# Masked attention on one core: scores and product with V moved from halves of TensorE's array to 64x64 quarters

## The chip, the cores and the metric

The kernel runs on one core of one Trainium2 chip. The metric is the device time of one execution in microseconds (us); several executions are quoted as their median. All runs quoted here are in the fast state. The profile is of one further execution. Engines are named as the profile does: PE (TensorE's matmuls), PEld (its weight loads), DVE (VectorE), ACT (ScalarE), POOL (GpSimd), SP (the queue that issues transfers).

## The reference, cut to what matters

```python
x = _layernorm(x + graph_convolution_with_batchnorm(x, adj, ...))     # layer 0
qkv = x @ W                                                           # layer 1: 4 heads of 64
scores = einsum('bhid,bhjd->bhij', q, k) / sqrt(64) + where(adj == 0, -inf, 0)
out = einsum('bhij,bhjd->bhid', softmax(scores), v)
x = _layernorm(x + out)
```

x is 8 x 2048 x 256 in fp32. The change touches layer 1 alone, which takes the last 2631 of the 4072 us.

## The kernel before

The work is cut into 64 units: a batch, a pair of heads (128 of the 256 columns) and a chunk of 512 queries. A unit has 16 key tiles `j` of 128 keys, taken two at a time in 8 steps `g`. Scores run two steps ahead of the product.

```python
ps_s = ctx.enter_context(tc.tile_pool(name="ps_s", bufs=2, space=PSUM))   # 2 banks each
ps_o = ctx.enter_context(tc.tile_pool(name="ps_o", bufs=2, space=PSUM))   # 1 bank each
ps_m = ctx.enter_context(tc.tile_pool(name="ps_m", bufs=2, space=PSUM))   # 1 bank each

# scores(u, g)                               two heads on the array's upper and lower 64 rows
ps = ps_s.tile([P, 2, CH], F32, name="ps_s")
for h in range(2):
    hs = slice(h * HD, (h + 1) * HD)
    nc.tensor.matmul(ps[:, h, :], kt[hs, j * P : (j + 1) * P], qt[hs, k * CH : (k + 1) * CH],
                     start=True, stop=True)
# ...
nc.vector.tensor_tensor(pt, ps, mask[...], op=ALU.subtract)              # DVE, 1.2 us
nc.scalar.activation(pt, pt, AF.Exp, scale=2.0**MASK_EXP)                # ACT, 1.05 us
nc.gpsimd.tensor_add(accs[u, q], accs[u, q], pt)                         # POOL, 2.36 us, 14 a unit

# weigh(u, g)                                two heads on the array's left and right 64 columns
for h in range(2):
    nc.tensor.matmul(outs[u][h * HD : (h + 1) * HD, :], qkv[b, hp][2][:, j, h * HD : (h + 1) * HD],
                     pt[:, h, :], start=(j == 0), stop=(j == NT - 1))

def finish_copy(u):                          # the way out, one step after the unit's last product
    ot = ap_.tile([P, CH], F32, name="ot")
    nc.scalar.copy(ot, outs[u])
```

Beside these steps stand projections, transposes and two layer norms per chunk. One belongs to the next batch's rows, one to the finished rows. Each layer norm has this chain, and it matters below:

```python
nc.vector.tensor_scalar(rs, mv[:, :, 1], EPS, None, op0=ALU.add)         # DVE
nc.gpsimd.tensor_tensor(rs, rs, mhalf[:, :TPC], op=ALU.pow)              # POOL
nc.vector.scalar_tensor_tensor(nm, mv[:, :, 0], -1.0, rs, ...)           # DVE
nc.scalar.activation(t[:, i, :], t[:, i, :], AF.Identity, bias=nm, scale=rs)   # ACT, four times
```

The compiler chooses the order of each engine's instructions, and the traces show that an edit in one place can move instructions elsewhere (an instance at 2118 us is given at the end of the part on why the prediction was wrong). They also show an engine waiting for the next instruction in its order while a later one could run (VectorE at 3944 us, below); the text calls that order the engine's queue.

## Time and profile before

| | us |
|---|---|
| time, median of 3 runs | 4072.4 |
| attention, from first score to end | 2631 |
| PE busy, share of the whole | 97% |
| POOL busy in the attention's steady period | 273 of 324 |

"Steady period" is the stretch of eight units of one batch, which repeats every 323.8 us. Read busy shares as follows. A TensorE that is 97% busy by modelled ends can still hide pauses, so the argument here rests on the times at which matmuls start. The prediction shows the lines.

### The profile page before, as it was taken

The page shows a single profiled execution, that of the slowest core. Times are in us where ns is not written, and L with a number is a line of the kernel's source. Part 1 is how long each engine was busy: PE and PEld are TensorE (multiplying, and loading weights), DVE is VectorE, ACT ScalarE, POOL GpSimd, SP SyncE. Part 2 cuts the span into 40 slices and gives each one's busy share as a digit, 9 for nine tenths or more (in the row PEclk, how much of TensorE's full clock was granted, in tenths as well). Part 3 has the DMA queues.
Part 4 walks back from the last instruction along what each step waited for, and adds up shares of the span by engine and source line. Part 5 has one row for each costly group of instructions (what it writes and reads, how often), then busy time and mean ns, then how long its engine had stood idle before and what let it go on. Part 6 is the DMA issues. An engine that isn't in the chain of part 4 may idle for free. (4 is left out here: it accounts for less than half of the span.)

```text
span 4072.3 us, 38096 instructions
## 1 busy us (share of the span) xinstructions
PE 3938.3 (97%) x14626; PEld 1559.8 (38%) x14626; DVE 1867.2 (46%) x2525; ACT 1665.7 (41%) x2077; POOL 2285.9 (56%) x1083
## 2 busy tenths in 40 slices
PE   7999999999989989999999999999999999999997
PEld 5444444444434433333333333333333333333332
DVE  5211111111124435665565665665656666556565
ACT  5000000000024345555555555555555555545554
POOL 0011101110100038887887887888888888788897
PEclk8999999999999989999999999999999999999998
DMA  5111101110147620000010000000000000000000
GB/s 217 64 45 52 52 31 49 47 49 31 47 158 230 208 68 21 25 28 26 16 42 21 21 32 21 32 32 21 32 21 32 26 27 27 26 6 26 6 1 22
DMA packets 94426, 197.28 MB, mean 48 GB/s; under 512 B 7072, under 2 KB 73120, under 8 KB 83872
## 3 DMA queue, kind: packets, MB, share of 16 engines
q1 hardware_dynamic: 94240, 194.80, 13.7%
q8 instruction: 117, 1.92, 0.2%
q14 instruction: 69, 0.57, 0.0%
HBM read 106.70 MB, written 88.08 MB: 48 GB/s over the span
## 5 line engine op out<-in xcount | busy, mean ns | idle before, releaser
L466 POOL TENSOR_TENSOR acc<-acc,pt 128x1024 f32<-128x1024 f32 x768 | 1814.2, 2362 | 329.1 <-ACT pt L459 286.5
L453 DVE TENSOR_TENSOR pt<-ps_s,mask 128x1024 f32<-128x1024 f32 x1024 | 1209.4, 1217 | 943.5 <-PE ps_s L446 908.4
L459 ACT ACTIVATE pt<-pt 128x1024 f32<-128x1024 f32 x1024 | 1066.5, 1054 | 816.7 <-DVE pt L453 796.2
L446 PE MATMUL ps_s<-qt,kt 64*128 64x512 f32 x4096 | 1041.1, 620 | 47.8 <-DVE pt L453 47.7
L475 PE MATMUL ps_o<-pt,v 128*64 128x512 f32 x4096 | 1013.0, 607 | 2.9 <-ACT pt L459 2.9
L209 PE MATMUL pa<-at,xb 128*128 128x512 f32 x2048 | 885.5, 592 | 0.0
L446 PEld LDWEIGHTS ps_s<-qt,kt 64*128 64x128 f32 x4096 | 351.3, 186 | 640.1 <-issue 339.9
L187 POOL TENSOR_SCALAR xb<-xb,dinv 128x256 f32<-128x256 f32 x112 | 103.0, 948 | 863.9 <-DMA xb<-in_x_dram 851.8
L209 PEld LDWEIGHTS pa<-at,xb 128*128 128x128 f32 x2048 | 389.0, 190 | 487.2 <-issue 480.0
L475 PEld LDWEIGHTS ps_o<-pt,v 128*64 128x64 f32 x4096 | 252.0, 136 | 637.6 <-issue 539.8
L242 ACT ACTIVATE h<-ph,b1s 128x512 f32<-128x512 f32 x128 | 87.9, 687 | 993.9 <-PE ph L235 993.9
L228 DVE TENSOR_TENSOR ag<-pa,dbc 128x512 f32<-128x512 f32 x64 | 44.3, 692 | 769.8 <-PE pa L209 769.8
L464 POOL TENSOR_TENSOR acc<-pt 128x1024 f32<-128x1024 f32 x128 | 302.3, 2362 | 71.4 <-ACT pt L459 70.2
L414 PE MATMUL pm<-x1t,wq 128*128 128x512 f32 x512 | 255.7, 624 | 0.5 <-ACT x1t L398 0.5
L295 PE MATMUL py<-h,w2s 128*128 128x512 f32 x512 | 223.6, 599 | 13.7 <-ACT h L287 13.7
L235 PE MATMUL ph<-ag,w1s 128*128 128x512 f32 x512 | 225.1, 592 | 0.0
L88 POOL TENSOR_TENSOR rs<-rs,mhalf 128x4 f32<-128x4 f32 (+1 forms) x2 | 1.7, 870 | 378.9 <-DVE rs L87 378.9
L350 ACT ACTIVATE x<-x,ln_nm,ln_rs 128x256 f32<-128x256 f32 x256 | 132.6, 588 | 100.0 <-DVE ln_nm L346 100.0
L243 DVE BATCH_NORM_STATS2 st<-h 128x6 f32<-128x512 f32 x128 | 88.8, 694 | 148.5 <-ACT h L242 148.5
L414 PEld LDWEIGHTS pm<-x1t,wq 128*128 128x128 f32 x512 | 88.4, 191 | 165.7 <-issue 104.9
L295 PEld LDWEIGHTS py<-h,w2s 128*128 128x128 f32 x512 | 98.4, 193 | 138.9 <-issue 119.1
L287 ACT ACTIVATE h<-h,sh,sc 128x512 f32<-128x512 f32 x128 | 93.3, 801 | 134.9 <-DMA h<-h_d 125.3
(78 smaller groups left out, 1780.7 us busy)
## 6 DMA issues: line engine op xcount, KB each, us to landing
h_d<-h SPq DMA_DIRECT2D x32, 1024.0 KB, 3.9
h<-h_d SPq DMA_DIRECT2D x32, 1024.0 KB, 5.9
a<-in_adj_dram SPq DMA_DIRECT2D x16, 1024.0 KB, 8.3
xb<-in_x_dram SPq DMA_DIRECT2D x32, 512.0 KB, 3.9
y_d<-y SPq DMA_DIRECT2D x32, 512.0 KB, 6.4
yt<-y_d SPq DMA_DIRECT2D x32, 512.0 KB, 3.3
x<-in_x_dram SPq DMA_DIRECT2D x32, 512.0 KB, 3.8
x_d<-x SPq DMA_DIRECT2D x32, 512.0 KB, 2.8
```

The costliest lines, as they stand in the source:

```text
L187: nc.gpsimd.tensor_scalar(t4[:, j, :], t4[:, j, :], dv, None, op0=ALU.mult)
L209: nc.tensor.matmul(pa, xs[b][m // TPC][:, m % TPC, d * P : (d + 1) * P], at[:, m, c * CH : (c + 1) * CH], start=(m == 0), stop=(m == NT - 1),)
L235: nc.tensor.matmul(ph, w1s[:, d, f * P : (f + 1) * P], ag[:, d, :], start=(d == 0), stop=(d == ND - 1),)
L295: nc.tensor.matmul(py, w2s[:, f, o * P : (o + 1) * P], h[:, f, :], start=(f == 0), stop=(f == NH - 1),)
L350: nc.scalar.activation(t[:, i, :], t[:, i, :], AF.Identity, bias=nm[:, i : i + 1], scale=rs[:, i : i + 1],)
L414: nc.tensor.matmul(pm, wq[:, d, wcols], xt[:, d, cols], start=(d == 0), stop=(d == ND - 1))
L446: nc.tensor.matmul(ps[:, h, :], kt[hs, j * P : (j + 1) * P], qt[hs, k * CH : (k + 1) * CH], start=True, stop=True,)
L453: nc.vector.tensor_tensor(pt, pss[j - g * GJ], mask[:, j, None, k * CH : (k + 1) * CH].to_broadcast([P, 2, CH]), op=ALU.subtract,)
L459: nc.scalar.activation(pt, pt, AF.Exp, scale=2.0**MASK_EXP)
L464: nc.gpsimd.tensor_add(accs[u, q], probs[u, j - 1], pt)
L466: nc.gpsimd.tensor_add(accs[u, q], accs[u, q], pt)
L475: nc.tensor.matmul(outs[u][h * HD : (h + 1) * HD, :], qkv[b, hp][2][:, j, h * HD : (h + 1) * HD], pt[:, h, :], start=(j == 0), stop=(j == ...
```

## The change

Its intent: scores use the array as two row halves, the product as two column halves, so the array changes its tiling twice a step. On quarters both have one tiling. A product over quarters splits its 128 keys over two row tiles, which write to two PSUM banks; they are added on the way out. Two banks per output leave room for one output buffer in place of two.

```diff
-        ps_o = ctx.enter_context(tc.tile_pool(name="ps_o", bufs=2, space=PSUM))
+        ps_o = ctx.enter_context(tc.tile_pool(name="ps_o", bufs=1, space=PSUM))
...
-                for h in range(2):
-                    nc.tensor.matmul(ps[:, h, :], kt[hs, j * P : (j + 1) * P], qt[hs, ...], ...)
+                for q in range(2):
+                    for h in range(2):
+                        nc.tensor.matmul(ps[q * HD : (q + 1) * HD, h, :], kt[hs, c0 : c0 + HD], qt[hs, ...], ...)
...
-                outs[u] = ps_o.tile([P, CH], F32, name="ps_o")
+                outs[u] = ps_o.tile([P, 2, CH], F32, name="ps_o")
...
                 for h in range(2):
-                    nc.tensor.matmul(outs[u][h * HD : (h + 1) * HD, :], qkv[b, hp][2][:, j, ...], pt[:, h, :], ...)
+                    for q in range(2):
+                        nc.tensor.matmul(outs[u][h * HD : (h + 1) * HD, q, :], qkv[b, hp][2][qs, j, ...], pt[qs, h, :], ...)
...
-            nc.scalar.copy(ot, outs[u])
+            nc.scalar.copy(ot, outs[u][:, 0, :])
+            nc.vector.tensor_add(ot, outs[u][:, 1, :], ot)
```

More of the change, by code (lines that the diff above doesn't have):

```diff
@@ L443, in scores @@
                 ps = ps_s.tile([P, 2, CH], F32, name="ps_s")
-                for h in range(2):
-                    hs = slice(h * HD, (h + 1) * HD)
-                    nc.tensor.matmul(
-                        ps[:, h, :], kt[hs, j * P : (j + 1) * P], qt[hs, k * CH : (k + 1) * CH],
-                        start=True, stop=True,
-                    )
+                for q in range(2):
+                    for h in range(2):
+                        hs = slice(h * HD, (h + 1) * HD)
+                        c0 = j * P + q * HD
+                        nc.tensor.matmul(
+                            ps[q * HD : (q + 1) * HD, h, :],
+                            kt[hs, c0 : c0 + HD],
+                            qt[hs, k * CH : (k + 1) * CH],
+                            start=True,
+                            stop=True,
+                        )
                 pss.append(ps)
@@ L474, in weigh @@
                 for h in range(2):
-                    nc.tensor.matmul(
-                        outs[u][h * HD : (h + 1) * HD, :],
-                        qkv[b, hp][2][:, j, h * HD : (h + 1) * HD],
-                        pt[:, h, :],
-                        start=(j == 0),
-                        stop=(j == NT - 1),
-                    )
+                    for q in range(2):
+                        qs = slice(q * HD, (q + 1) * HD)
+                        nc.tensor.matmul(
+                            outs[u][h * HD : (h + 1) * HD, q, :],
+                            qkv[b, hp][2][qs, j, h * HD : (h + 1) * HD],
+                            pt[qs, h, :],
+                            start=(j == 0),
+                            stop=(j == NT - 1),
+                        )
         def finish_copy(u):
             ot = ap_.tile([P, CH], F32, name="ot")
-            nc.scalar.copy(ot, outs[u])
+            nc.scalar.copy(ot, outs[u][:, 0, :])
+            nc.vector.tensor_add(ot, outs[u][:, 1, :], ot)
             outs[u] = ot
```

## The prediction

> **What bounds the kernel now.** I read the page first, then the windows by stage, then the order of the weight loads on TensorE, then the ends of a few units, and last the table of waits. The page's busy shares and costliest groups:
>
> ```profile
> PE 3938.3 (97%) x14626; PEld 1559.8 (38%) x14626; DVE 1867.2 (46%) x2525; ACT 1665.7 (41%) x2077; POOL 2285.9 (56%) x1083
> ...
> L466 POOL TENSOR_TENSOR acc<-acc,pt 128x1024 f32<-128x1024 f32 x768 | 1814.2, 2362 | 329.1 <-ACT pt L459 286.5
> L453 DVE TENSOR_TENSOR pt<-ps_s,mask 128x1024 f32<-128x1024 f32 x1024 | 1209.4, 1217 | 943.5 <-PE ps_s L446 908.4
> L459 ACT ACTIVATE pt<-pt 128x1024 f32<-128x1024 f32 x1024 | 1066.5, 1054 | 816.7 <-DVE pt L453 796.2
> L446 PE MATMUL ps_s<-qt,kt 64*128 64x512 f32 x4096 | 1041.1, 620 | 47.8 <-DVE pt L453 47.7
> L475 PE MATMUL ps_o<-pt,v 128*64 128x512 f32 x4096 | 1013.0, 607 | 2.9 <-ACT pt L459 2.9
> ```
>
> The reader should see that TensorE is busy 97% and that the two groups the change touches are half of that. Both use half the array per matmul, and both already run two at a time: 4096 records of 620 ns would be 2540 us, yet their union is 1041. Each fp32 matmul leaves two records, so 2048 matmuls of each kind. The attention runs from 1441 us (first score) to the end, some 2620 us. Busy ends are modelled, though, so a busy TensorE can hide gaps. Starts cannot. A long chain in one shape (the aggregation) starts one record every 0.43 us:
>
> ```profile
> 900.24 0.19 PEld L209 LDWEIGHTS pa<-at,xb 128*128 128x128 f32 x1 [0.24 <-issue]
> 900.67 0.19 PEld L209 LDWEIGHTS pa<-at,xb 128*128 128x128 f32 x1 [0.24 <-issue]
> 901.10 0.19 PEld L209 LDWEIGHTS pa<-at,xb 128*128 128x128 f32 x1 [0.24 <-issue]
> ```
>
> and one scores run followed by one product run:
>
> ```profile
> 2402.14 0.30 PEld L446 LDWEIGHTS ps_s<-qt,kt 64*128 64x128 f32 x4 [0.81 <-DVE pm L519]
> 2402.68 0.19 PEld L446 LDWEIGHTS ps_s<-qt,kt 64*128 64x128 f32 x2 [0.24 <-issue]
> 2403.11 0.19 PEld L446 LDWEIGHTS ps_s<-qt,kt 64*128 64x128 f32 x2 [0.23 <-issue]
> 2404.06 0.20 PEld L475 LDWEIGHTS ps_o<-pt,v 128*64 128x64 f32 x4 [0.76 <-issue]
> 2404.55 0.14 PEld L475 LDWEIGHTS ps_o<-pt,v 128*64 128x64 f32 x2 [0.28 <-issue]
> 2404.97 0.14 PEld L475 LDWEIGHTS ps_o<-pt,v 128*64 128x64 f32 x2 [0.28 <-issue]
> ```
>
> A run is four pairs of records, ideally 4 x 0.43 = 1.72 us. The scores run takes 2404.06 - 2402.14 = 1.92. Its 0.20 of loss is in two places: first to second pair 0.53 instead of 0.43, and last pair to the next run also 0.53. In the product run the first step is 0.48 to 0.49. These steps repeat throughout the attention (medians over all runs 534, 480 and 525 to 529 ns against 429). So TensorE is the bound, and roughly a tenth of its attention time is lost where the shape changes.
>
> TensorE is not the bound in the last batch, whose late units have no projections beside them:
>
> ```profile
> 3878.63:3910.93 32.30, 32.30 (x146) 10.40 (x144) 20.52 (x20) 17.77 (x20) 31.36 (x14) 1.00 0.00 1
> 3910.93:3943.23 32.30, 32.30 (x146) 10.40 (x144) 20.52 (x20) 17.76 (x20) 31.36 (x15) 1.00 0.00 1
> 3943.23:3983.80 40.57, 34.39 (x146) 10.78 (x144) 25.61 (x30) 19.61 (x23) 38.86 (x18) 0.92 0.04 14
> ```
>
> The columns are the window, its length, then PE, PEld, DVE, ACT and POOL busy. POOL is at 97%. A unit needs 14 of its 2.36 us additions, 33.1 us, which is over 32.3; the debt is paid in the third window, where TensorE stands for 6 us.
>
> **What the Trainium skill says.** "TensorEngine Tiling (Array Packing)", Key Properties: changing the tiling mode, not just the tile, drains TensorE. The trace agrees: last pair to next run costs 0.10 us extra at every change of shape, nothing within one. "TensorE: Matmul & The Clock Gate", LDWEIGHTS: the load lasts by its columns, P/1.2 ns. The trace agrees: after a drain the first step is 105 ns longer with 128 columns and 51 with 64, against 107 and 53. The same page, Part 3, says row and column tiles compose. No run here has both, but the sum of the probabilities runs on four column tiles:
>
> ```profile
> 2515.68 0.16 PEld L495 LDWEIGHTS pm<-acc,ones 128*32 128x32 f32 x8 [0.76 <-issue]
> 2516.67 0.20 PEld L475 LDWEIGHTS ps_o<-pt,v 128*64 128x64 f32 x4 [0.84 <-issue]
> ```
>
> Eight loads start within 0.16 us and the whole lasts 0.99 us, two record times plus the drain, so four fp32 tiles do run at once. "PSUM — Partial Sum Buffer", PSUM bank collisions: different row tiles must not write one bank at the same time. That is why the output needs two banks, hence one buffer instead of two.
>
> **The change part by part.**
> 1. Matmuls. Each is cut into a quarter of the array; per key tile there are four, two records each, instead of two. If four run at once, a key tile still takes 2 x 0.43 us. The array's work is unchanged: zero gain, zero cost.
> 2. Drains. Scores and product now have one shape. In order of time, 347 of the 512 scores runs are followed at once by a product run, and each such border saves 0.10 of drain and 0.05 of exposed load: 52 us. 275 product runs are followed at once by a scores run; 23 of these stood over 1 us anyway, and the other 252 save 0.10 + 0.105: 52 us. The other 237 scores runs still follow a 128-wide step but load 64 columns instead of 128: 0.054 each, 13 us. Sum 117 us. The last seven of 64 units are bound by POOL, so 57/64 of it: 104 us.
> 3. Second half on the way out. One more VectorE operation on 128x512 per unit. The kernel's like additions from PSUM take about 0.69 us; 64 of them make 44 us, and VectorE is only some 60% busy in the attention. Its own time is hidden.
> 4. One output buffer. The next unit's first product must now wait for copy, then addition. A unit's end:
>
> ```profile
> 1773.28 1.99 PE L446 MATMUL ps_s<-qt,kt 64*128 64x512 f32 x8
> 1773.82 0.19 PEld L446 LDWEIGHTS ps_s<-qt,kt 64*128 64x128 f32 x2 [0.24 <-issue]
> 1774.09 0.57 ACT L485 COPY ot<-ps_o 128x512 f32<-128x512 f32 x1
> 1774.25 0.19 PEld L446 LDWEIGHTS ps_s<-qt,kt 64*128 64x128 f32 x2 [0.23 <-issue]
> 1774.53 2.35 DVE L453 TENSOR_TENSOR pt<-ps_s,mask 128x1024 f32<-128x1024 f32 x2 [1.50 <-PE ps_s L446]
> 1775.20 0.20 PEld L475 LDWEIGHTS ps_o<-pt,v 128*64 128x64 f32 x4 [0.76 <-ACT ot L485]
> ```
>
> The copy ends at 1774.66, the addition could end at 1775.40 and the product start at 1775.45, where it started at 1775.20 and, without drains, wants to some 0.35 earlier: a stall of 0.55 us. If VectorE takes the next subtraction first (it began at 1774.53), 1.1 us more. The units repeat in a period of eight. Reading each boundary this way: three have a projection or transposes and over 1.4 us of slack after the copy, no stall; one has 1.65 us but VectorE full of layer norm, some 0.3 to 0.5; two are like the one shown, 0.55 to 1.65 each; in two the copy comes after the next product has begun, 1.8 to 2.6 each. Sum 5.4 to 9 us per period, times seven: 38 to 63, middle 48.
> 5. POOL's pow of the layer norm queues behind its additions, and VectorE and then TensorE wait for it (49 us of VectorE's time in the attention). A faster TensorE leaves POOL further behind: I charge 6 us.
>
> Net 104 - 48 - 6 = 50 us: 4072 - 50 = 4022, rounded to 4020.
>
> **The rivals.**
> - *Drains alone matter.* The new wait falls into time TensorE would have spent otherwise. For it: POOL and VectorE have slack that lets them catch up during a stall. Against it: in four of eight boundaries the copy demonstrably ends too late. It gives about 4072 - 104 = 3968.
> - *The wait eats it all.* If the addition goes behind two subtractions or the layer norm, 2.5 us at five boundaries of eight make 88 us, with point 5 nothing is left: 4065 to 4080.
> - *Quarters don't overlap fully.* Twice the instructions: 32 records in 3.43 us, 54 ns each. For it: the densest stretch in the trace, the transposes at the start, shows 54.6 ns per record, and nothing longer is faster. Against it: those are limited by their 128 columns, and the sums issue 16 records in far less. With two at a time a key tile would double and the time go to 5800; a small issue limit, 10% of the attention's 1.76 ms of score and product starts, gives 4200.
> - *POOL becomes the bound everywhere.* In the steady period it has 273 us in 324. Eight units of 33.1 make 265, so it stays under the new period of about 316. It would take a gain of over 45 us per period; not reached.
>
> **Range and chances.** The drain gain is well supported (90 to 120), the stalls are the loose term (0 to 100). I take 3968 to 4070. Faster by over 2% means under 3991, which needs stalls under about 20 us: 0.22. Slower by over 2% needs the quarters to fail: 0.12. Within 2%: 0.66.
>
> **What would show it.** Right: scores to product starts 0.43 us apart where they touch, a run of 1.72, four records starting together; drains left only at 128-wide and 32-wide steps. At unit borders TensorE's loads of the product wait for the new VectorE addition, about 45 us in all. The last units keep their length of some 34 us. Wrong: starts of four records spread over more than 0.43 us (the third rival); no wait on the addition (the first); waits on it over 2 us at most borders (the second).

## The result, and the profile after

The changed kernel takes 4068.4 us (4 runs, 4065.4 to 4070.1) against 4074.4 for the kernel before beside it. The ratio is 0.9985, with a 95% interval of 0.9968 to 1.0002. Ratios are the mean time of one kernel's fast runs over that of the other's of the same rounds, so they are not quite the ratio of the medians. The time lies inside the range, but the change is within the noise, where a gain of 50 us was forecast.

In the profile after, the same source lines have other numbers: scores are L449 (L446 before), the product L484 (L475), the subtraction L459, the exponential L465, POOL's additions L470 and L472, the copy out L494, the new addition L495. The page's groups that answer to those shown of before:

```profile
PE 3855.4 (95%) x22818; PEld 1544.6 (38%) x22818; DVE 1883.5 (46%) x2589; ACT 1667.1 (41%) x2077; POOL 2288.4 (56%) x1083
...
L449 PE MATMUL ps_s<-qt,kt 64*64 64x512 f32 x8192 | 1021.8, 606 | 81.2 <-DVE pt L459 79.5
L484 PE MATMUL ps_o<-pt,v 64*64 64x512 f32 x8192 | 1009.6, 600 | 41.4 <-DVE ot L495 41.4
```

There are twice the records, in nearly the same busy time, and TensorE as a whole is busy 83 us less. Its idle time before these two groups, by contrast, has grown from 47.8 and 2.9 us to 81.2 and 41.4. The end of a product run, a scores run and the start of the next product run, by their weight loads:

```profile
2117.07 0.15 PEld L484 LDWEIGHTS ps_o<-pt,v 64*64 64x64 f32 x4 [0.28 <-issue]
2117.50 0.15 PEld L449 LDWEIGHTS ps_s<-qt,kt 64*64 64x64 f32 x4 [0.28 <-DVE ri L524]
...
2118.79 0.15 PEld L449 LDWEIGHTS ps_s<-qt,kt 64*64 64x64 f32 x4 [0.28 <-issue]
2119.22 0.15 PEld L484 LDWEIGHTS ps_o<-pt,v 64*64 64x64 f32 x4 [0.28 <-issue]
```

Each line is four loads that start together; two lines are left out between the second and the third, at 2117.93 and 2118.36. So the groups come every 0.43 us, straight across both borders. The quarters overlap fully, and the drain is gone: the change does what it was made for. To see where the gain went, I took the starts of all matmuls in the attention from both traces. From each step between one start (or group that starts together) and the next I subtracted what the step takes in a long chain: 0.43 us, or 0.11 for a transpose and the short matmuls of V's projection. What is left, added up by kind:

| over the plain step, us in the whole attention | before | after | difference |
|---|---|---|---|
| up to 0.16 each: drains and exposed loads | 253.8 | 138.1 | -116 |
| longer, from scores to product | 1.7 | 47.0 | +45 |
| longer, to scores or from scores to side work | 67.7 | 99.3 | +32 |
| 0.16 to 0.5 each: steps at half clock, and short waits | 11.5 | 42.0 | +31 |
| the rest (end of the kernel and others) | 18.8 | 16.5 | -2 |

The sum is -10, while the attention in fact shrank by 6. Most of this rest is the counting's own: where four quarters did not quite start together they make one group more, and the changed kernel has ten more groups (6795 against 6785), each charged 0.43 us. The 116 us were real, and three kinds of pause gave 108 of them back. In the fourth row, the clock's own record puts 30 of the 42 us and 7 of the 11.5 at half clock; the others are short waits, most of them of scores for VectorE.

**The first kind** is the wait for the output buffer. This is the boundary where it is longest, once in each period:

```profile
2055.40 2.06 ACT L350 ACTIVATE x<-x,ln_nm,ln_rs 128x256 f32<-128x256 f32 x4
...
2057.37 1.04 ACT L465 ACTIVATE pt<-pt 128x1024 f32<-128x1024 f32 x1
...
2058.31 0.80 ACT L367 ACTIVATE yt<-yt,sh,sc 128x512 f32<-128x512 f32 x1
...
2059.02 0.56 ACT L494 COPY ot<-ps_o 128x512 f32<-128x512 f32 x1
...
2059.61 0.69 DVE L495 TENSOR_TENSOR ot<-ps_o,ot 128x512 f32<-128x512 f32 x1 [3.96 <-ACT ot L494]
...
2060.36 2.54 PE L484 MATMUL ps_o<-pt,v 64*64 64x512 f32 x16 [3.50 <-DVE ot L495]
```

The copy is ready to go when the unit's product ends near 2053, but stands in ScalarE's queue behind an exponential, the layer norm's four scalings, another exponential and a batch norm. VectorE stands idle 3.96 us for it, then TensorE stands 3.50 by modelled ends (3.68 by starts). In the kernel before, the same copy was as late and held up nobody: the next product wrote to the other buffer and had started already.

```profile
2059.70 1.94 PE L475 MATMUL ps_o<-pt,v 128*64 128x512 f32 x8
...
2060.29 0.56 ACT L485 COPY ot<-ps_o 128x512 f32<-128x512 f32 x1
```

**The second kind** is the wait behind POOL. The longest is in the last batch:

```profile
3943.20 1.10 DVE L344 TENSOR_SCALAR ln_rs<-ln_mv 128x4 f32<-128x4 f32 x1
...
3951.48 4.76 POOL L472 TENSOR_TENSOR acc<-acc,pt 128x1024 f32<-128x1024 f32 x2
3956.20 1.02 POOL L345 TENSOR_TENSOR ln_rs<-ln_rs,mhalf 128x4 f32<-128x4 f32 x1
3957.25 0.17 DVE L346 SCALAR_TENSOR_TENSOR ln_nm<-ln_mv,ln_rs 128x4 f32<-128x4 f32 x1 [12.95 <-POOL ln_rs L345]
...
3958.60 1.98 PE L449 MATMUL ps_s<-qt,kt 64*64 64x512 f32 x8 [14.40 <-DVE pt L459]
```

VectorE hands POOL the layer norm's variance at 3944.3, but POOL must first work off the additions that it is behind with, and starts the small pow at 3956.20. VectorE has the next operation of the layer norm at the head of its queue and waits 12.95 us. The subtraction that would free a score buffer stands behind it, and TensorE waits 14.40. The pow acts as a barrier: at most of the 64 layer norms (42 waits in the lists below) VectorE, and often TensorE after it, waited until POOL had caught up. The waits for it over the whole attention, before and then after:

```profile
ACT x L350 <- DVE ln_nm L346: 94.0, 48, 6.0
...
DVE ln_nm L346 <- POOL ln_rs L345: 54.6, 33, 4.7
```

```profile
ACT x L350 <- DVE ln_nm L346: 201.8, 48, 16.8
...
DVE ln_nm L346 <- POOL ln_rs L345: 74.5, 42, 13.0
...
PE ps_o L484 <- DVE ot L495: 41.4, 34, 3.5
```

The columns are the total, the number of waits and the longest. ScalarE, which waits for VectorE, which waits for POOL, stood 108 us longer; the last line is the first kind of pause. TensorE's own pauses of this kind are the third row of the table, and most of them (98 of the 99 us after, 59 of the 68 before) lie beside a layer norm's chain on VectorE, from the addition of epsilon to the product with the mean, or start no more than 1.5 us after it. About half of the growth falls in the last batch: from the product of unit 57 (of 0 to 63) to the end, the changed kernel took 275.0 us against 266.9, although 15 us of drains had gone there too. Even before POOL sees the request the chain can wait for it. The addition of epsilon, a 128x4 operation, took 0.16 us at its fastest, 1.23 in the median and 2.07 at most in the changed kernel, and a long one ended when POOL's running addition ended (2120.55 + 1.64 = 2122.19, against 2117.36 + 4.79 = 2122.15). The Trainium skill, "SBUF — State Buffer", Who interferes with whom, says that such VectorE operations can share a port pair with GpSimd, and that the one that comes second is blocked for the whole instruction. The trace agrees with that, and with six of fourteen additions cut (an experiment below) the median was 0.17.

**The third kind** is a slower clock behind some of the long pauses. The lines are windows around the 3.7 us pause at 2056, behind the 14.6 us pause at 3944 and, in a block of its own, behind a pause of 3.7 us at 1735. The columns are the window, its length, the busy time of PE, PEld, DVE, ACT and POOL, the granted clock, then two on DMA:

```profile
2056.20:2060.30 4.10, 0.66 (x8) 0.00 (x0) 0.69 (x2) 4.10 (x8) 3.55 (x2) 1.00 0.36 128
2060.30:2065.20 4.90, 4.84 (x32) 1.67 (x36) 2.82 (x4) 2.59 (x3) 3.06 (x3) 0.65 0.02 3
...
3958.60:3962.80 4.20, 4.20 (x20) 1.24 (x24) 2.75 (x3) 3.65 (x5) 2.19 (x1) 0.50 0.35 125
```

```profile
1738.90:1742.30 3.40, 3.40 (x32) 1.23 (x36) 2.73 (x3) 2.49 (x3) 1.64 (x2) 1.00 0.02 5
```

The clock was 0.65 and 0.50 behind the first two pauses, and 1.00 again in the next windows (2065 to 2080 and 3963 to 3972); behind the third it stayed at 1.00. The stretches at half clock lasted 3.41 us or a multiple of it (the last, which the kernel's end cuts, apart), and one of 3.41 us adds 0.42 us to about four steps, some 1.7 us in all. The Trainium skill, "TensorE: Matmul & The Clock Gate", Part 1, says that the clock falls to half after an idle window of about 3.4 us and stays there about as long. The trace agrees on how long it stays, and only in part on what brings it on. Between 1600 and 3900 us the changed kernel has 21 pauses of 2.6 to 3.7 us, and the clock fell behind 13 of them: behind five of six of 3.67 to 3.69 us, but also behind four of seven of 2.69. It fell behind none of 2.1 or of about 1 us there. In the kernel before, at 2056 to 2060, there was no pause (PE busy 4.10 of 4.10 at clock 1.00).

### The profile page after: what moved, and what is told of

Read it like the earlier page. It is cut to its first block, busy times and chain, and to the rows that moved or that the text cites. A ratio compares the mean times of both kernels' runs of the same rounds, so it can differ in the third digit from the quotient of the medians.

```text
span 4068.3 us, 54545 instructions
## 1 busy us (share of the span) xinstructions
PE 3855.4 (95%) x22818; PEld 1544.6 (38%) x22818; DVE 1883.5 (46%) x2589; ACT 1667.1 (41%) x2077; POOL 2288.4 (56%) x1083
## 5 line engine op out<-in xcount | busy, mean ns | idle before, releaser
L472 POOL TENSOR_TENSOR acc<-acc,pt 128x1024 f32<-128x1024 f32 x768 | 1816.2, 2365 | 320.8 <-ACT pt L465 272.9
L459 DVE TENSOR_TENSOR pt<-ps_s,mask 128x1024 f32<-128x1024 f32 x1024 | 1208.6, 1219 | 791.7 <-PE ps_s L449 765.2
L465 ACT ACTIVATE pt<-pt 128x1024 f32<-128x1024 f32 x1024 | 1069.4, 1055 | 769.7 <-DVE pt L459 743.5
L449 PE MATMUL ps_s<-qt,kt 64*64 64x512 f32 x8192 | 1021.8, 606 | 81.2 <-DVE pt L459 79.5
L484 PE MATMUL ps_o<-pt,v 64*64 64x512 f32 x8192 | 1009.6, 600 | 41.4 <-DVE ot L495 41.4
L449 PEld LDWEIGHTS ps_s<-qt,kt 64*64 64x64 f32 x8192 | 287.1, 134 | 655.4 <-issue 427.9
L484 PEld LDWEIGHTS ps_o<-pt,v 64*64 64x64 f32 x8192 | 299.5, 134 | 613.3 <-issue 506.8
L470 POOL TENSOR_TENSOR acc<-pt 128x1024 f32<-128x1024 f32 x128 | 302.9, 2366 | 83.3 <-ACT pt L465 83.3
```

What stands on the lines that cost most here:

```text
L449: nc.tensor.matmul(ps[q * HD : (q + 1) * HD, h, :], kt[hs, c0 : c0 + HD], qt[hs, k * CH : (k + 1) * CH], start=True, stop=True,)
L459: nc.vector.tensor_tensor(pt, pss[j - g * GJ], mask[:, j, None, k * CH : (k + 1) * CH].to_broadcast([P, 2, CH]), op=ALU.subtract,)
L470: nc.gpsimd.tensor_add(accs[u, q], probs[u, j - 1], pt)
L484: nc.tensor.matmul(outs[u][h * HD : (h + 1) * HD, q, :], qkv[b, hp][2][qs, j, h * HD : (h + 1) * HD], pt[qs, h, :], start=(j == 0), stop=( ...
```

## The experiments

The theories: **B**, the single output buffer and its way out; sharpened after the first runs to **C**, the copy is late because it stands in ScalarE's queue. **Q**, POOL's queue sets the pace; sharpened to **P**, it does so through the layer norm's pow. A third possibility stood beside them: that quarters cost something which starts don't show. All kernels that keep the arithmetic gave right results; those that cut it gave wrong ones on purpose.

### POOL's additions cut, in both kernels

```diff
-                elif r:
+                elif r % 2:
                     nc.gpsimd.tensor_add(accs[u, q], accs[u, q], pt)
...
-            nc.scalar.copy(sums[u], pm)
+            nc.scalar.activation(sums[u], pm, AF.Copy, bias=1.0)
```

This leaves 8 of 14 additions per unit; the constant keeps sums from being zero.

> The kernel before with 8 instead of 14 of POOL's 2.36 us additions per unit (sums wrong on purpose, every other instruction kept; a constant 1 is added to the sums so that none is zero). Theory Q (the gain is lost to POOL's queue: layer norm's pow[...]): the few stalls of the old kernel that come from POOL go, 7 us per period of eight units and some 10 at the end, so 40 to 60 us faster than before, near 4020. Theory B (the gain is lost to the single output buffer): the same number, since the old kernel has two buffers; this run is the base for the next.

> The changed kernel with the same cut of POOL's additions. Theory Q: of the 19 us of TensorE stalls per period only the 6 to 7 at the output buffer stay, and the 15 us stall of the last batch goes, so near 3950, and 60 to 80 us below the old kernel with the same cut. Theory B: it falls no more than the old kernel did, to about 4015, level with the old kernel with the same cut.

Measured: 4000.5 (old) and 3980.0 (changed), against 4074.9 for the kernel before. The old kernel fell by 74 us, more than the 40 to 60 that both theories gave it, so POOL had been a hidden limit all along. The changed one came out between the two theories: it is only 20 us better than the old one even now. In its trace, 49 us of waits from scores to product remain. Neither theory alone is right.

### The single buffer in the old shapes

```diff
-        ps_o = ctx.enter_context(tc.tile_pool(name="ps_o", bufs=2, space=PSUM))
+        ps_o = ctx.enter_context(tc.tile_pool(name="ps_o", bufs=1, space=PSUM))
...
-            nc.scalar.copy(ot, outs[u])
+            nc.scalar.activation(ot, outs[u], AF.Copy, scale=0.5)
+            nc.vector.scalar_tensor_tensor(ot, outs[u], 0.5, ot, op0=ALU.mult, op1=ALU.add)
```

> The kernel before, old shapes, with one output buffer that is emptied by a ScalarE copy (times 0.5) and then a VectorE operation that adds the other 0.5 (result right, same two steps and same wait as in the change). Theory B: 40 to 60 us slower than before, near 4125. Theory Q: 10 to 25 us slower, near 4095, because the wait alone is short and the old kernel has slack in it.

Measured: 4091.9, ratio 1.0044 (1.0027 to 1.0061), 17 us slower. Waits from scores to product rose from 1.7 to 23.9 us. That is inside what theory Q gave it (10 to 25) and well short of theory B's 40 to 60: a miss for B. With drains in the way the same buffer costs about half of what it costs the changed kernel (47 us); that the old TensorE comes to it later is the likely reason, and no run shows it alone.

### Both halves taken out by ScalarE at once

```diff
-            nc.scalar.copy(ot, outs[u][:, 0, :])
-            nc.vector.tensor_add(ot, outs[u][:, 1, :], ot)
+            nc.scalar.copy(ot, outs[u])          # both halves
...
+            ot = o2[:, 0, :]                     # later, in finish(u)
+            nc.vector.tensor_add(ot, ot, o2[:, 1, :])              # both in SBUF
```

> The changed kernel, both halves copied out by one ScalarE operation, the addition made later in SBUF, so that the output buffer is free some 0.7 us earlier and does not wait for VectorE. Theory B: 30 to 50 us faster than the changed kernel, near 4025. Theory Q: under 15 us, since TensorE only comes to POOL's queue sooner.

Measured: 4111.5, 43 us slower than the changed kernel: a miss for both theories. At the boundary shown above the copy still started behind the same ScalarE work, now took 0.99 us, and TensorE still waited 3.20 us. The addition, which now reads two operands in SBUF, took 1.28 us in the median and up to 2.68, where the one that reads PSUM took 0.69. Over the attention the waits from scores to product did fall, from 47.0 to 23.7 us: the short ones behind VectorE's addition went, the long ones behind ScalarE stayed. But waits from product to scores grew from 54 to 89 us, and steps of 0.16 to 0.5 us over from 42 to 72 (46 of these at half clock). So the miss pointed to ScalarE's queue as what makes the way out late where it is latest. Where the new waits come from it does not show, since VectorE's order changed too (TensorE's did not).

### Both halves taken out by VectorE

```diff
-            nc.scalar.copy(ot, outs[u][:, 0, :])
+            nc.vector.tensor_copy(ot, outs[u][:, 0, :])
             nc.vector.tensor_add(ot, outs[u][:, 1, :], ot)
```

Here the compiler left the orders on TensorE, POOL and the transfer queue exactly as in the changed kernel, which makes it the cleanest of the experiments on the buffer.

> The changed kernel with the first half also copied out by VectorE, so that the way out does not pass through ScalarE's queue; TensorE's, POOL's and the DMA queue's orders stay as they are. Theory C (the single buffer is emptied late because its copy stands in ScalarE's queue behind exponentials and layer norm[...]): the 47 us of waits from scores to product fall to under 15 and half of the 42 us at half clock go, so 40 to 60 us faster than the changed kernel, near 4015. Theory Q (POOL's queue sets the pace, whatever else is taken away): under 15 us.

> The same with POOL's additions cut to 8 of 14 (wrong sums on purpose). Theory C: 50 to 70 us below the changed kernel with that cut, near 3920, and 75 to 90 below the old kernel with that cut, which is most of the 116 us that the drains gave back. Theory Q or one of the compiler's ordering: within 20 us of 3980.

> Control: the kernel before with its copy moved from ScalarE to VectorE. Theory C: with two buffers nobody waits for the copy, so within 10 us of the kernel before. If moving work from ScalarE to VectorE is itself a gain, it is 20 us or more faster.

Measured: 4051.7, and with POOL's additions cut 3926.1; the control, the old kernel with its copy on VectorE, 4071.7 (ratio 0.9999), as expected. The same boundary, with the copy now in VectorE's queue:

```profile
2055.11 0.68 DVE L494 COPY ot<-ps_o 128x512 f32<-128x512 f32 x1
...
2055.83 0.69 DVE L495 TENSOR_TENSOR ot<-ps_o,ot 128x512 f32<-128x512 f32 x1
...
2056.66 1.90 PE L484 MATMUL ps_o<-pt,v 64*64 64x512 f32 x13 [0.25 <-DVE ot L495]
```

The way out starts 3.9 us earlier and TensorE waits 0.25 us in place of 3.50. Over the attention the waits from scores to product fell from 47.0 to 0.2 us. That is what theory C said. Yet the time fell by 17 us, not by 40 to 60: waits from product to scores rose from 54 to 77, and steps of 0.16 to 0.5 us over from 42 to 52 (the part at half clock stayed at 30 to 31). With POOL's additions cut the same edit brings 54 us (3980.0 to 3926.1), as theory C said. The two limits stand in series: take one away and TensorE arrives earlier at the other.

### Scores alone on quarters

The diff is the scores' part of the change; product, buffers and way out stay as before.

> Scores on quarters, product as before (128x64, two buffers, no addition). If a change of shape costs a drain and the exposed load goes by its columns, no border is saved but 512 first loads have 64 columns instead of 128, 0.054 us each: 15 to 30 us faster than the kernel before, near 4050. If quarters alone were the gain, 60 us or more; if twice the instructions cost something, slower.

Measured: 4069.5, ratio 0.9991 (0.9982 to 1.0000), a miss. Inside the trace the expected part is there: steps up to 0.16 us within one kind of matmul fell from 116 to 87 us, by 29 (I had 0.054 x 512 = 28). The borders stayed. But steps of 0.16 to 0.5 us over rose from 12 to 31 (at half clock from 7 to 19) and waits from product to scores by 4. A small gain on TensorE was given back just as the large one was.

### The layer norm's pow taken away

```diff
-            nc.vector.tensor_scalar(rs, mv[:, :, 1], EPS, None, op0=ALU.add)
-            nc.gpsimd.tensor_tensor(rs, rs, mhalf[:, :TPC], op=ALU.pow)
+            nc.vector.tensor_scalar(rs, mv[:, :, 1], 0.0, 0.4, op0=ALU.mult, op1=ALU.add)
```

POOL keeps all its additions and loses 64 operations of 1.02 us.

> The kernel before with POOL's pow of the layer norm taken away: VectorE writes a constant 0.4 in place of the inverse deviation, by the operation that added epsilon (wrong on purpose); POOL's additions all stay. Theory P (the pow at the end of POOL's queue makes VectorE, and then TensorE, wait until POOL has caught up): 15 to 35 us faster, near 4050. If POOL's sum of work is what counts: under 10 us.

> The changed kernel with the same cut. Theory P: 30 to 50 us faster than the changed kernel, near 4030, more than the old kernel gains, because its TensorE runs further ahead of POOL. POOL's sum of work: under 10 us.

> The changed kernel with both halves taken out by VectorE and the same cut. Theory P: 50 to 90 us below the same kernel with pow (4052), near 3980, since the waits that remained there, some 54 us more than in the old kernel from product to scores with the half clock behind them, begin at this pow. POOL's sum of work: within 15 us of 4050, and a cut of the additions is the only help.

Measured: 4031.9, 4014.1 and 3974.5. Theory P holds: taking away 65 us of POOL's 2288 gave 41, 54 and 77 us, and most where TensorE runs furthest ahead. The first two are more than I had expected, 15 to 35 and 30 to 50; under 10 or 15 would have spoken for POOL's sum of work. It is its queue in front of the pow. Two rivals fall with these traces. The small VectorE operation in front of it, kept with other constants, still took 1.22 us in the median in the changed kernel, so its slowness alone is not the barrier. And the compiler kept its order: against the kernel it was made from, each of the three has the same order on POOL, but for the pow, and on VectorE, but for one subtraction in the old kernel. (In the last batch POOL's sum does bind, as the prediction's windows showed.)

### Both of POOL's parts taken away

> The kernel before with both cuts (8 of 14 additions, no pow; wrong on purpose): nothing of POOL's is left to wait for. It had few waits left with the additions alone cut, so near 3995.

> The changed kernel with both cuts and both halves taken out by VectorE. If the drains are real gain: 90 to 115 us below the old kernel with both cuts, near 3890. If the quarters have a cost of their own that the trace's starts don't show: no better than the 74 us of the pair with the additions alone cut.

Measured: 3991.9 and 3902.1, 90 us apart, the low end of what I had expected if the drains were real gain. In the old kernel's trace 2 us of waits longer than 0.5 us are left in the attention (the end of the kernel apart), in the changed one's 14. All pairs together, in us:

| | POOL as it is | no pow | additions cut | both cut |
|---|---|---|---|---|
| old shapes | 4074 | 4032 | 4000 | 3992 |
| quarters, as changed | 4068 | 4014 | 3980 | not run |
| quarters, way out on VectorE | 4052 | 3975 | 3926 | 3902 |
| old less last row | 22 | 57 | 74 | 90 |

The third possibility falls with this table: quarters have no large cost of their own. Of the 116 us, 90 show once hardly anybody has to wait. Of the rest, 13 us are steps of 0.16 to 0.5 us over (16.4 against 3.2; only 2 us of them at half clock, most of the others short waits for VectorE) and 12 the waits just named.

### A right version that beats both

```diff
             nc.vector.tensor_scalar(rs, mv[:, :, 1], EPS, None, op0=ALU.add)
+            nc.vector.tensor_scalar(nm, mv[:, :, 0], -1.0, None, op0=ALU.mult)
             nc.gpsimd.tensor_tensor(rs, rs, mhalf[:, :TPC], op=ALU.pow)
-            nc.vector.scalar_tensor_tensor(nm, mv[:, :, 0], -1.0, rs, op0=ALU.mult, op1=ALU.mult)
+            nc.gpsimd.tensor_tensor(nm, nm, rs, op=ALU.mult)
```

VectorE now only sends to POOL and never waits for it in a layer norm.

> The changed kernel, both halves taken out by VectorE, right result: the product of mean and inverse deviation moves from VectorE to POOL, so that VectorE's queue no longer waits for POOL's pow and only ScalarE does, which has two steps of slack. Theory P: 20 to 60 us below 4052, near 4010; POOL has 8 us more work per period. POOL's sum of work: 0 to 10 us slower than 4052.

> The kernel before with the product of mean and inverse deviation on POOL (right result), control of the version at 4009. Theory P: 10 to 30 us faster than before, near 4052, so that the quarters with the mended way out are worth some 45 us on top. If the layer norm alone made the gain: near 4010.

Measured: 4009.0 with quarters and the way out on VectorE (ratio 0.9843, 0.9826 to 0.9859), 4032.1 with the old shapes (0.9903, 0.9887 to 0.9920). Both results are right. The layer norm alone is worth 40 us to the old kernel, more than I had expected, and the quarters with the way out on VectorE 23 more, half of the 45 that I had expected. What still holds this version up can be read from its waits:

```profile
ACT x L349 <- POOL ln_nm L347: 442.1, 63, 17.9
...
PE ps_o L483 <- ACT pt L464: 32.8, 10, 8.0
```

The barrier has moved from VectorE to ScalarE. There most waits for POOL are absorbed, but ten times the exponential came so late that the product waited, 32.8 us in all. The longest, 8.0 us, is in the last batch, where POOL is short of time itself: from unit 57 to the end this version takes 274.9 us, as the changed kernel did (275.0).

## Why the prediction was right or wrong

- **Part 1, matmuls: right.** Four quarters start together every 0.43 us; the third rival (quarters that don't overlap, or a limit on issue) is refuted. Its "32 records in 3.43 us" is a slip: a step has 32 matmuls and 32 loads, and only the 64 together make 54 ns each.
- **Part 2, drains: right.** 117 us were forecast for all units, 116 left the trace. I had taken off the last seven units as unchanged, and that was wrong: three of them did shorten, from 32.3 to 30.6 us each, and then waits, the longest of 14.6 us, took back more than that. The stretch from unit 57 to the end came out 8 us longer.
- **Part 3, the addition's own time: right.** It takes 0.69 us each, 44 us in all, hidden.
- **Part 4, the single buffer: right in total.** 48 us were forecast and 45 measured. Two boundaries of a period were to cost 0.55 to 1.65 us each and took 0.71 and 0.65. Two with a late copy were to cost 1.8 to 2.6 each; one took 3.68, the other 2.08 or some 0.5 by turns, so that the total is right partly by luck. What could make a wait longer I looked for in VectorE's queue; the longest came from the copy's place in ScalarE's.
- **Part 5 is the term that failed.** I charged 6 us for "A faster TensorE leaves POOL further behind". The pauses of that kind measured +32 us, about half of it in the last batch. The experiments show why it is no small correction: the pow ties TensorE to POOL at the layer norms, so that what TensorE gains between two of them it can lose at the next; without the pow the changed kernel is 54 us faster.
- **Missing altogether:** steps of 0.16 to 0.5 us over, +31 us. About 23 of them are the half clock behind some of the longer pauses, the rest short waits. I had counted a pause at its length only.
- **The rivals.** The second one ("The wait eats it all", 4065 to 4080) named the right size by the wrong path, which is luck: not 2.5 us at five boundaries, but the wait as forecast, with POOL's barrier and the clock beside it. The argument against "POOL becomes the bound everywhere" compared sums over a period, 265 us of additions under 316. The 265 are the additions alone; all of POOL's work is 273, as the same passage says, which leaves 43 us and not 51. But the margin was not what failed: the queue with the pow in it held TensorE up well before its sum was used up.

With the measured terms the prediction's sum would have been 116 - 45 - 32 - 31 = 8 us of gain, where 6 were measured. That it closes is no test, since the terms come from the same two traces. The time lies inside the stated range by 2 us, and that is luck too: the range was wide because of the stalls at the output buffer, which came out as forecast, and other terms used it up.

What stays open: how much of the growth of the waits comes from the compiler's order. In one stretch of the kernel before, VectorE's order had two subtractions between the layer norm's operations (2118.4 and 2119.8), in the changed kernel none, and its pause there is 3.30 us in place of 0.63. The runs that kept the order of the kernel they were made from show both waits to be real, but no run gave the kernel before and the changed one a common order. Nor does any run here show what decides behind which pauses the clock falls.

## What to carry to other kernels

When a bound engine is made faster, look for every place where another engine's queue makes it wait in turn: a small operation at the end of a long queue, in the middle of a chain that the bound engine needs, is a barrier, whatever the busy shares say. When an output loses its second buffer, ask in whose queue its copy will stand. Try the gain once in a pair of runs, old and new, with the suspected queue cut short, wrong result and all; that shows whether the gain is lost or only hidden.

## What the Trainium skill lacked or had wrong

- "TensorEngine Tiling (Array Packing)" says that a change of tiling drains TensorE, but not what it costs. Here each change cost 0.10 us, and 0.05 (64 columns) or 0.105 us (128 columns) more for the first load that nothing hid.
- No page says what fp32 matmuls, which leave two records of 0.43 us each in the trace, do on quarters. Here four of 64x64 started within about 0.02 us and ran fully at once, at 0.43 us for each of the two records.
- "SBUF — State Buffer" gives the rule for VectorE and GpSimd, not its size for small operations. Here a 128x4 operation of 0.16 us took 1.23 us in the median beside POOL's 2.36 us additions (0.17 with six of fourteen cut), and a 128x512 addition from SBUF took 1.28 in place of the 0.69 of one that reads PSUM.
- "TensorE: Matmul & The Clock Gate", Part 1, names an idle window of about 3.4 us as what halves the clock. Here it was halved behind four of seven pauses of 2.69 us as well, and not behind one of six of 3.7. What the page doesn't add up is the price of one such fall: some 1.7 us on top of the pause itself, 30 us of this kernel's attention against 7 before.
